# Layer 1's products of the last 64 tokens, in three groups over four PSUM banks

## The chip, the cores and the metric

The kernel runs on one core of a Trainium2 chip. The metric is the device time of one execution in microseconds (us). The engines are TensorE (PE, with its weight loads written PEld), VectorE (DVE), ScalarE (ACT), GpSimd (POOL) and SyncE (SP, which here issues most of the DMAs).

## The reference

Four layers follow each other on an input of 4 x 56 x 56 x 256 numbers in fp32; each adds to its input what it computes from the group-normalised input. Layers 0, 2 and 3 are forms of windowed attention and aren't touched. Layer 1 takes each image's 3136 pixels as tokens:

```python
xn = x / jnp.maximum(jnp.linalg.norm(x, axis=-1, keepdims=True), EPS)
A = jnp.einsum('bnc,cc,bmc->bnm', xn, W_adj, xn)
A = jnp.exp(5.0 * (A - jnp.max(A, axis=-1, keepdims=True)))
A = A * (1.0 - jnp.eye(n, dtype=A.dtype))
A = A / jnp.maximum(jnp.sum(jnp.abs(A), axis=-1, keepdims=True), EPS)
...
AxW = jnp.einsum('bnc,dc->bnd', Ax, W_aff)
diff = rowsum * (xW + b_aff) - AxW
```

A layer norm and a leaky ReLU of `diff` follow. The sum over all pairs of tokens is the bulk of the work: 3136 x 3136 logits, their exponentials, and the product of these with the values, for each of four images.

## The kernel before

**Tiles and symmetry.** The 3136 tokens are 24 tiles of 128 (`NB`) and a rest of 64 (`REST`). The matrix of exponentials is symmetric, so only tiles with j <= i are computed, and each block serves twice: transposed, as a part of row j's sum (the "row product"), and as it stands, as a part of row i's sum (the "column product"). The values `xw` have 257 columns, the last of them -1, so that the same product gives the sum of the weights. Row j's sum stays in a PSUM bank for the whole row; column products go each to a bank of its own and are added at once to `acc` in SBUF by `add_up` (L1562 to L1567): the first one into a tile is copied, by DVE or ACT, and later ones are added by DVE.

**The rest.** The last 64 tokens have their own three units an image, `q` = 0, 1, 2, each against eight tiles. `rest_logits` (L1570) puts the logits of 64 tokens against two groups of four tiles on the two halves of the partitions: `a` = 0 on partitions 0 to 63, `a` = 1 on 64 to 127. `rest_transposed` (L1589) transposes the four 128 x 128 blocks into bank t, from which ACT copies them to `at`. `rest_products` (L1597) then does, for each i of 0 to 3, two column products (one for each half, on 64 rows of the array, written 64*128 in the profile, L1603), their addition, and two row products (on 64 columns of the array, 128*64, L1607), which build up both halves of the bank `po`. For q = 2 a product of the rest with itself follows (`own`, L1611). `po` is added to `racc` (L1613, L1615).

**PSUM.** [...]`psum_tile(tag, bufs)` (L872) gives the next of `bufs` buffers under a tag; a matmul into a buffer waits until the readers of its last use are through. In layer 1 the eight banks are: s (logits, 2), t (transposes, 1), v (column products, 2), o (row products, 2) and m (1, by `ps_m`), which the smaller steps of tokens, statistics and output use.

**What sets the order.** A list of `units` (L1733 and after) holds the blocks of each row, four tiles at a time, with the rest units put in: q = 0 and q = 1 of image 0 at the very start and of the later images between rows 20 and 22 of the image before; q = 2 after row 0 of its own image. The main loop (L1793) does for each unit: a small step (`small_step`, which is one of lengths, values, output transposes, statistics), the transposes, the next unit's logits (`begin`), another small step, then the products. `tick` (L1554), called between products, emits one of the pending steps of normalisation (`normal`, `leaky`, the next image's tokens), mostly on DVE. In layer 1 PE and DVE execute in the order in which the code emits (`manual_schedule`, engines PE and DVE); a scheduler orders ACT's, POOL's and SP's lists.[...]

## Time and profile before

| | |
|---|---|
| median of 3 runs | 3770.52 us (3767.21 to 3772.34) |
| the profiled execution | 3769.93 us, span 3768.0 us |
| layer 1, about | 734 to 2600 us |
| PE busy in it (734 to 2600) | 1852.76 of 1866.00 us |
| DVE, ACT, POOL busy in it | 866.46, 420.53, 538.36 us |
| L1603, column products of the rest | 192 records, 377 to 481 ns, median 429 |
| L1607, row products of the rest | 192 records, 380 to 432 ns, median 406 |
| L1567, first copies out of a bank | DVE 64 at 426 ns, ACT 32 at 374 ns (medians) |
| L1564, additions to `acc` | DVE 1104 at 423 ns (median) |

The span runs from the first to the last instruction. Each fp32 product is two records on PE. [...]records of matmuls that follow each other overlap; the distance from start to start is what a product takes up of PE. In brackets after a row stands how long its engine had nothing to do before it, and whose end ended that.

### The profile page before, as it was taken

The page shows a single profiled execution, that of the slowest core. Times are in us where ns is not written, and L with a number is a line of the kernel's source. Part 1 is how long each engine was busy: PE and PEld are TensorE (multiplying, and loading weights), DVE is VectorE, ACT ScalarE, POOL GpSimd, SP SyncE. Part 2 cuts the span into 40 slices and gives each one's busy share as a digit, 9 for nine tenths or more (in the row PEclk, how much of TensorE's full clock was granted, in tenths as well). Part 3 has the DMA queues.
Part 4 walks back from the last instruction along what each step waited for, and adds up shares of the span by engine and source line. Part 5 has one row for each costly group of instructions (what it writes and reads, how often), then busy time and mean ns, then how long its engine had stood idle before and what let it go on. Part 6 is the DMA issues. An engine that isn't in the chain of part 4 may idle for free. (4 is left out here: it accounts for less than half of the span.)

```text
span 3768.0 us, 112324 instructions
## 1 busy us (share of the span) xinstructions
PE 3665.8 (97%) x48826; PEld 2478.1 (66%) x48826; DVE 2200.9 (58%) x4188; ACT 1472.2 (39%) x3125; POOL 1815.9 (48%) x1966
## 2 busy tenths in 40 slices
PE   8999999999999999999999999999999999999998
PEld 4555556677776777767777667775666666555554
DVE  5777777634445444464344544445676777777676
ACT  5565566422222222222222222222666666444443
POOL 4777777612235222352222421123777777555555
PEclk9999999999999999999999999999999999999999
DMA  6544444300010000011000000002544444534443
GB/s 213 169 153 134 132 123 137 134 7 23 23 27 29 22 19 18 21 32 28 19 16 22 26 20 10 11 20 78 138 133 137 132 128 119 155 126 139 130 134 99
DMA packets 278039, 304.94 MB, mean 81 GB/s; under 512 B 33624, under 2 KB 268764, under 8 KB 277084
## 3 DMA queue, kind: packets, MB, share of 16 engines
q1 hardware_dynamic: 275680, 297.43, 25.7%
q8 instruction: 385, 6.31, 0.7%
q0 software_dynamic: 1568, 0.16, 0.1%
q14 instruction: 118, 0.97, 0.1%
q10 hardware_dynamic: 288, 0.08, 0.0%
HBM read 205.04 MB, written 92.55 MB: 79 GB/s over the span
## 5 line engine op out<-in xcount | busy, mean ns | idle before, releaser
L1564 DVE TENSOR_TENSOR acc<-acc,ps_v 128x257 f32<-128x257 f32 x1104 | 463.8, 422 | 781.8 <-PE ps_v L1642 753.4
L1642 PE MATMUL ps_v<-xw,e 128*128 128x257 f32 x2208 | 611.0, 381 | 3.4 <-DVE xnT L1509 2.2
L1637 PE MATMUL ps_o<-xw,at 128*128 128x257 f32 x2208 | 609.0, 379 | 0.0
L1532 PE MATMUL ps_s<-xnT,xd 128*128 128x512 f32 (+3 forms) x1344 | 571.4, 548 | 3.9 <-DVE xnT L1509 3.9
L1626 ACT COPY at<-ps_t 128x512 f32<-128x512 f32 (+3 forms) x332 | 170.6, 514 | 960.9 <-PE ps_t L1623 960.7
L1642 PEld LDWEIGHTS ps_v<-xw,e 128*128 128x128 f32 x2208 | 413.4, 189 | 144.6 <-issue 83.2
L1087 POOL TENSOR_TENSOR b<-e 126x336 f32<-126x336 f32 (+5 forms) x512 | 499.5, 997 | 7.7
L1637 PEld LDWEIGHTS ps_o<-xw,at 128*128 128x128 f32 x2208 | 419.1, 190 | 60.1
L952 PE MATMUL ps_m<-xn,w_wqkv 128*32 128x392 f32 x4096 | 376.4, 496 | 8.0 <-ACT gst L917 3.4
L1525 POOL TENSOR_SCALAR xd<-xnT,vec 128x128 f32<-128x128 f32 x192 | 116.4, 616 | 478.0 <-PE ps_s L1532 477.8
L1078 POOL TENSOR_TENSOR e<-e,m0t 126x672 f32<-126x672 f32 (+3 forms) x128 | 238.8, 1865 | 182.1 <-ACT e L1077 180.6
L1535 ACT ACTIVATE e<-ps_s 128x512 f32<-128x512 f32 x336 | 185.4, 552 | 355.0 <-PE ps_s L1532 351.8
L1532 PEld LDWEIGHTS ps_s<-xnT,xd 128*128 128x128 f32 x1344 | 225.4, 191 | 141.4 <-issue 126.2
L1078 POOL TENSOR_TENSOR e<-e,bias 119x784 f32<-119x784 f32 (+5 forms) x128 | 239.4, 1870 | 157.3 <-ACT e L1077 156.9
L1096 PEld LDWEIGHTS ps_o<-e,vp 124*32 124x32 f32 (+3 forms) x8192 | 200.3, 110 | 101.9 <-issue 84.1
L998 ACT ACTIVATE no<-rs 128x168 f32<-128x168 f32 (+2 forms) x256 | 94.0, 367 | 426.0 <-DVE rs L1960 190.2
L952 PEld LDWEIGHTS ps_m<-xn,w_wqkv 128*32 128x32 f32 x4096 | 123.8, 110 | 183.1 <-issue 128.6
L1960 DVE RECIPROCAL rs<-ps_o 128x196 f32<-128x196 f32 (+2 forms) x128 | 175.7, 1372 | 109.7 <-PE ps_o L1096 108.0
L1096 PE MATMUL ps_o<-e,vp 124*32 124x112 f32 (+3 forms) x8192 | 232.2, 249 | 3.1 <-POOL e L1078 2.5
L1075 ACT ACTIVATE e<-e 126x672 f32<-126x672 f32 (+5 forms) x256 | 219.7, 858 | 13.3 <-DVE e L1074 1.9
L1077 ACT ACTIVATE e<-ps_s 126x672 f32<-126x672 f32 (+5 forms) x256 | 206.3, 806 | 5.4 <-PE ps_s L1067 3.0
L979 PE MATMUL ps_m<-w_wqkv,xn 128*32 128x256 f32 x3136 | 196.9, 381 | 2.1 <-DVE v L983 1.6
(214 smaller groups left out, 5945.5 us busy)
## 6 DMA issues: line engine op xcount, KB each, us to landing
x<-xr SPq DMA_DIRECT2D x64, 392.0 KB
x<-in_x SPq DMA_DIRECT2D x53, 448.0 KB
x<-x SPq DMA_DIRECT2D x60, 392.0 KB
xr<-x SPq DMA_DIRECT2D x60, 392.0 KB
vd<-v SPq DMA_DIRECT2D x72, 256.0 KB
xr<-in_x SPq DMA_DIRECT2D x32, 392.0 KB
xr<-x SPq DMA_DIRECT2D x28, 448.0 KB
x<-xr SPq DMA_DIRECT2D x28, 448.0 KB
```

The costliest lines, as they stand in the source:

```text
L952: nc.tensor.matmul(pm[j * HD:(j + 1) * HD, :n], lhsT=w[:, h, col + j * HD:col + (j + 1) * HD], rhs=rhs(h), start=(h == 0), stop=(h == CC - 1))
L979: nc.tensor.matmul(pm[i:i + HD, j * C:(j + 1) * C], lhsT=xn[:, h, first + i:first + i + HD], rhs=w[:, h, :], start=(h == 0), stop=(h == CC ...
L1075: nc.scalar.activation(ev, ev, AF.Exp)
L1077: nc.scalar.activation(ev, sv, AF.Exp)
L1078: nc.gpsimd.tensor_tensor(parts(ev), parts(ev), w["emask"], ALU.mult)
L1087: nc.gpsimd.tensor_tensor(w["b"][a][:nk, :, :2 * nq].rearrange("p h (i c) -> p h i c", i=2), ev[:, :, :, 0, :], ev[:, :, :, 1, :], ALU.add)
L1096: nc.tensor.matmul(w["o"](k, i)[j * HD:(j + 1) * HD], lhsT=ones[:nk, :HD] if k else v(j, u), rhs=w["b"][j // 2][:nk, j % 2, i * nq:(i + 1) ...
L1532: nc.tensor.matmul(s[:, :n], lhsT=xd[j][:, h, :], rhs=xnT[:, h, first * P:last * P], start=(h == 0), stop=(h == CC - 1))
L1535: nc.scalar.activation(e[:, :n], s[:, :n], AF.Exp, scale=5.0)
L1564: nc.vector.tensor_tensor(acc[:, i, :], acc[:, i, :], pv[:, :C + 1], ALU.add)
L1637: nc.tensor.matmul(out[j][:, :C + 1], lhsT=e[:, col(i)] if i == j else at[:, col(i)], rhs=xw[:, i, :], start=(i == j), stop=(i == NB - 1))
L1642: nc.tensor.matmul(pv[:, :C + 1], lhsT=e[:, col(i)], rhs=xw[:, j, :], start=True, stop=True)
```

## The change

`rest_products` alone is changed. Before, its order is, four times: two column products into the two v banks, their additions, two row products, a tick. After, it is: the column products of tiles i = 0 (into both v banks) and i = 1 (`a` = 0 into bank t, `a` = 1 into bank m), the four additions; all eight row products, with a tick after the second and the fourth pair; the column products of i = 2 (into t and m) and i = 3 (into v), their four additions; two ticks. The number of products, additions and ticks is the same, and so is every result's place.

```diff
         def rest_products(b, q, e, own, at):
             po = psum_tile("o", 2)
+
+            def by_column(i, banks):
+                for a, bank in enumerate(banks):
+                    pv = psum_tile(*bank)
+                    half = slice(a * REST, (a + 1) * REST)
+                    nc.tensor.matmul(pv[:, :C + 1], lhsT=e[half, i * P:(i + 1) * P], rhs=xw[half, NB, :], start=True, stop=True)
+                    found.append((i, a, pv))
+
+            def add():
+                for i, a, pv in found:
+                    add_up(b, 8 * q + 4 * a + i, pv, (nc.vector.tensor_copy, nc.scalar.copy)[a])
+                found.clear()
+
+            found, pair, others = [], [("v", 2)] * 2, [("t", 1), ("m", 1)]
+            by_column(0, pair)
+            by_column(1, others)
+            add()
             for i in range(4):
-                pv = [psum_tile("v", 2) for a in range(2)]
-                for a in range(2):
-                    half = slice(a * REST, (a + 1) * REST)
-                    nc.tensor.matmul(pv[a][:, :C + 1], lhsT=e[half, i * P:(i + 1) * P], rhs=xw[half, NB, :], start=True, stop=True)
-                for a in range(2):
-                    add_up(b, 8 * q + 4 * a + i, pv[a], (nc.vector.tensor_copy, nc.scalar.copy)[a])
                 for a in range(2):
                     nc.tensor.matmul(po[a * REST:(a + 1) * REST, :C + 1], lhsT=at[:, i * P + a * REST:i * P + (a + 1) * REST],
                                      rhs=xw[:, 8 * q + 4 * a + i, :], start=(i == 0), stop=(i == 3 and (a == 1 or own is None)))
+                if i % 2:
+                    tick()
+            by_column(2, others)
+            by_column(3, pair)
+            add()
+            for _ in range(2):
                 tick()
             if own is not None:
```

## The prediction

> **What bounds the kernel now.** First the page: its parts 1 and 2 say that TensorE (PE) is busy nearly throughout, and part 5 puts the layer in question between the products on L1637 and L1642. The chain of waits on the page reaches back only into layer 3, so it doesn't speak of this stage. I therefore read busy time by stretches: layer 1 runs from about 734 to 2600 us.

> ```profile
> span 3768.0 us, 112324 instructions
> ...
> PE 3665.8 (97%) x48826; PEld 2478.1 (66%) x48826; DVE 2200.9 (58%) x4188; ACT 1472.2 (39%) x3125; POOL 1815.9 (48%) x1966
> ```

> The busy times of two stretches of layer 1 (microseconds, and records in brackets):

> ```profile
> core 0: us, PE busy (x) PEld busy (x) DVE busy (x) ACT busy (x) POOL busy (x), PEclk, DMA share, GB/s
> 734.00:800.00 66.00, 65.08 (x311) 40.35 (x310) 23.88 (x62) 21.16 (x41) 12.59 (x21) 1.00 0.27 106
> 800.00:1190.00 390.00, 389.27 (x1719) 292.95 (x1719) 178.45 (x460) 86.56 (x160) 115.94 (x165) 1.00 0.09 24
> ```

> In 800 to 1190 us PE is busy 389.27 of 390.00 us, and DVE, the next engine, 178.45. So the stage is PE's queue played back to back: a microsecond taken out of it brings the end forward by a microsecond, provided that no other engine comes within reach. The changed code stands twelve times in it (three units for each of four images: 192 records on L1603 at 16 a unit).

> Next I read the timeline of such a unit. This is the first of image 1 (start, length, engine, line, count, and in brackets the idle time before it with its releaser):

> ```profile
> 1189.84 0.70 PE L1603 MATMUL ps_v<-xw,e 64*128 64x257 f32 x4
> 1190.47 0.20 PEld L1607 LDWEIGHTS ps_o<-xw,at 128*64 128x64 f32 x4 [0.33 <-ACT e L1535]
> 1190.48 0.65 PE L1607 MATMUL ps_o<-xw,at 128*64 128x257 f32 x4
> 1190.58 0.43 DVE L1567 COPY acc<-ps_v 128x257 f32<-128x257 f32 x1 [0.23 <-PE ps_v L1603]
> 1190.62 0.38 ACT L1567 COPY acc<-ps_v 128x257 f32<-128x257 f32 x1 [0.18 <-PE ps_v L1603]
> 1191.06 0.30 PEld L1603 LDWEIGHTS ps_v<-xw,e 64*128 64x128 f32 x4 [0.39 <-DVE acc L1567]
> 1191.06 0.70 PE L1603 MATMUL ps_v<-xw,e 64*128 64x257 f32 x4
> ```

> A pair of column products (tiles 64*128) takes from 1189.84 to 1190.48, 0.63 us; the pair of row products (128*64) from 1190.48 to 1191.06, 0.58. Before each the weight load sits idle 0.33 to 0.39 us. Four rounds of 1.22 make the unit 4.88 us. "PE busy" hides this[...].

> How much of it is work? The undivided products give the pace:

> ```profile
> 755.46 0.59 PE L1642 MATMUL ps_v<-xw,e 128*128 128x257 f32 x2
> ...
> 755.89 1.03 PE L1637 MATMUL ps_o<-xw,at 128*128 128x257 f32 x4
> ```

> Two more records cost 1.03 - 0.59 = 0.44, so one of 257 columns costs about 0.215. A product is two records, and two half-array tiles run side by side: a pair needs 2 x 0.215 = 0.43. What remains, 0.20 for a column pair and 0.15 for a row pair, is paid at each alternation. That pairs of one kind do follow each other without it is seen where the last tokens' logits run:

> ```profile
> 735.55 1.94 PE L1574 MATMUL ps_s<-xnT,xdr 128*64 128x512 f32 x8
> ```

> Eight records of 512 columns at 0.43 each would take 3.44 in a row; they take 1.94, that is four slots of 0.43 and one 0.22.

> [...]

> **The change part by part.** Durations are from the one profiled execution: span 3768.0 us, its own time 3769.93, which is 0.6 under the median of 3770.52; I take savings off the median.

> 1. Alternations. Before: eight groups a unit, 4 x 0.63 + 4 x 0.58 = 4.84 (seen: 4.88). After: columns, rows, columns: 16 slots x 0.215 = 3.44, and three starts, 0.20 + 0.15 + 0.20: 3.99. Saved 0.89 a unit, twelve times: 10.7 us. Nothing is recomputed; the number of matmuls is the same. Unknown: whether column pairs on 64 rows follow each other at 0.215, since before never has two in a row. Their weight loads take 0.18 each, but both tiles' run together (four in 0.30 in the row above), so a slot of 0.215 covers them. Bounds: nothing lost, or 0.1 for each of five joints, 6.0 us in all.[...] I take zero.

> 2. Waits inside a unit that the change removes. From first column to the next other instruction, the twelve units take 67.1 us by the timeline, of which 12 x 4.88 is the rhythm above and 4 x 0.58 the product with `own` (L1611). The other 6.2 are waits:
>    - The third unit of each image (6.09 us instead of 5.46) adds all columns on DVE. The second and fourth columns wait for it twice, 0.31 each: "DVE acc L1564: 4.6, 12" among the releasers of L1603. With four banks, two pairs are emptied under the four row pairs (1.87 us): at 0.38 each the four adds, begun at 0.73, end at 2.3, and y's step on L1696 (0.41) at 2.7, while the banks are wanted at 2.93. Saved 4 x 0.63 = 2.5.
>    - The second unit of image 0 (6.21 us) waits 1.33 for ACT, which is filled from 744.28 to 751.56 with exponentials of layer 2's bias (L1849, 1.0 each). In the new order on ACT, m's first copy has one of these before it and should end near 748.2; its bank is wanted at 745.41 + 2.93 = 748.34. But m's and v's last copies come behind three more, near 751.9, and the next unit's second column wants v about then. I take 1.0 back of 1.33 (bounds 0 and 1.33).
>    - The second units of images 1 to 3 wait 0.74 at their second product for ACT's copy of `xw` (L961) out of v. That stays: 0.

> 3. Waits that the change adds. Bank t has one buffer, and so has m.
>    - At the end: the second group begins with t and m, and the next instruction on PE writes t (the transposes on L1623) or m. Column start to DVE's copy is 0.73, the copy 0.43, and 0.06 to PE: free at 1.22, wanted at 2 x 0.43 + 0.20 = 1.06. That is 0.16 behind which all PE waits, in eight units (the four with `own` have 0.58 more in between): 1.3 us. DVE is free in time: the steps moved between the copies (L945 0.60, L1701 0.55) end before 2.9 and t's copy comes at 3.66.
>    - At the beginning: t was emptied long before (L1594 ends some 0.5 us ahead of the unit, with another 0.53 before t's second use). m is late in the first unit, where ACT reads the statistics (L916, L917) until 738.5, wanted at 737.74 + 0.53: 0.3. In the first units of images 1 to 3 DVE's L1716 frees m at 1190.34, wanted at 1190.37: 0.
>    Together 1.6. Bounds: 0, where PE would not have been ready, and 1.1 per unit, 13, if each ACT copy of m stood behind an instruction of 1.06 us as in the second unit.

> 4. The rest. The tick steps move from after each tile to two in the middle and two at the end; PE and DVE keep the order in which the code emits. By the instruction lists of both kernels, SP and POOL, and so all DMA issues, keep their order; ACT's list differs by a copy to `at` that moves ahead of a square of 1.06 us (L1470). I cost this at nothing: ACT is idle 0.84 before most of its copies, and that cover gone would cost 0.4 a unit, already within the bound of 3.

> Sum: 10.7 + 2.5 + 1.0 - 1.6 = 12.6 us. 3770.5 - 12.6 = 3757.9; the profiled execution would be 3757.3. Layers 2 and 3 only begin earlier.

> **The rivals.**
> - *All of it comes*: no end waits (+1.3), the second unit's rest, and room downstream. 67.1 less 12 x 3.99 and 4 x 0.58 is 16.9: 3753.6. For it: PE bound. Against: the 0.74 on `xw` and the copy's 1.22 are in the trace.
> - *The joints don't close, or banks give part back*: 6.0 lost at the joints leaves 6.6, 3763.9; with as much again lost on t and m, 3770. For it: no row shows two row-tiled pairs in a row. Against: L1574 and the loads that run together.
> - *Slower: bank m behind ACT.* The second group's m product waits for ACT's copy of the first[...]. It decides from 1.05 us a unit on (12.6 / 12) and gives 0.2% slower from 1.7. At two bias exponentials a unit (2.0): 3757.9 + 24 = 3782. For it: the second unit has such a queue. Against: in the others ACT waits for the columns, not they for it.

> **How the numbers follow.** About 0.2%, 7.5 us, is what a measurement of this kernel can tell from no change. The forecast (3755 to 3761) 0.66; all of it 0.10; part given back (3761 to 3770) 0.20, of which 0.08 still faster by over 7.5; slower 0.04. Hence faster 0.84, same 0.12, slower 0.04. The range 3753.6 to 3764 takes in the first rival's end and the joints' bound.

> **What would show it.** Units near 4.15 us (4.6 with `own`), t's wait for DVE of about 0.16 ahead of the transposes, the weight load's idle time before row products once a unit instead of four times, layer 1 shorter by 12 to 13 us and layers 2 and 3 of the same length. I am wrong if column pairs in a group stand 0.5 or more apart, if releasers of the columns name ACT in most units, or if units shrink and PE idles by as much elsewhere.

## The result and the profile after

The changed kernel takes 3757.49 us (median of 7 runs, 3754.05 to 3760.45) against 3770.9 (7 runs) on the same chip: a ratio of 0.9965, 95% interval 0.9955 to 0.9974. That is 13 us, with an interval of 10 to 17. The forecast was 3757.9.

The page of the changed kernel, and then the busy times of stretches of layer 1:

```profile
span 3752.2 us, 112327 instructions
...
PE 3649.2 (97%) x48826; PEld 2480.3 (66%) x48826; DVE 2195.6 (59%) x4188; ACT 1471.4 (39%) x3125; POOL 1813.6 (48%) x1966
```

```profile
734.00:800.00 66.00, 65.86 (x327) 44.93 (x324) 25.75 (x69) 21.52 (x42) 12.30 (x20) 1.00 0.20 82
800.00:1180.00 380.00, 379.27 (x1678) 286.03 (x1677) 174.16 (x448) 83.64 (x154) 114.19 (x163) 1.00 0.09 24
```

The share of PE's busy time is what it was, 97%, and in the middle of layer 1 it idles 0.73 us as before. The number of PE records is the same. So the share tells nothing of the change; 16 us of "busy" have gone with the span.

Not all of these 16 us are the change's. I measure layer 1 in both traces from the first transposes of the rest (L1593) to the last logits (L1532): 1862.8 us before and 1850.8 after, 12.0 less. Layer 0, whose code is the same, took 735.0 and 730.9, and what follows layer 1 took 1170.3 and 1170.6. The traces' record of the granted clock has PE at half speed for 20.5 us of layer 0 before and 13.7 after; half of the difference, 3.4, is most of those 4.1 us. The traces of the experiments below bear this out: over all ten, this time runs from 10.2 to 23.9 us and the length of layer 0 with it, from 730.7 to 736.5. In layer 1 neither trace has such a stretch. Hence the length of layer 1 is a far sharper measure than the whole time, and I use both below.

The same unit as was shown of before, the first of image 1, PE's rows of the timeline:

```profile
1181.88 0.70 PE L1604 MATMUL ps_v<-xw,e 64*128 64x257 f32 x4
1182.41 0.38 PE L1604 MATMUL ps_t<-xw,e 64*128 64x257 f32 x1
1182.44 0.48 PE L1604 MATMUL ps_m<-xw,e 64*128 64x257 f32 x1
1182.63 0.38 PE L1604 MATMUL ps_t<-xw,e 64*128 64x257 f32 x1
1182.76 0.38 PE L1604 MATMUL ps_m<-xw,e 64*128 64x257 f32 x1
1183.06 1.96 PE L1618 MATMUL ps_o<-xw,at 128*64 128x257 f32 x16
1184.95 0.48 PE L1604 MATMUL ps_t<-xw,e 64*128 64x257 f32 x1
...
1185.28 0.38 PE L1604 MATMUL ps_t<-xw,e 64*128 64x257 f32 x1
...
1185.49 0.60 PE L1604 MATMUL ps_v<-xw,e 64*128 64x257 f32 x4
1186.17 0.44 PE L1640 MATMUL ps_t<-ident,e 128*128 128x128 f32 x2
```

The second column pair begins 0.53 after the first, the row products are one block of 1.89 us, start to start, and the unit ends after 4.29 instead of 4.88. Two small waits are to be seen, and the weight loads of this unit show both:

```profile
1182.20 0.40 PEld L1604 LDWEIGHTS ps_t<-xw,e 64*128 64x128 f32 x2
1182.43 0.29 PEld L1604 LDWEIGHTS ps_m<-xw,e 64*128 64x128 f32 x2
...
1184.95 0.18 PEld L1604 LDWEIGHTS ps_t<-xw,e 64*128 64x128 f32 x1 [0.39 <-issue]
...
1185.28 0.41 PEld L1604 LDWEIGHTS ps_v<-xw,e 64*128 64x128 f32 x4
1186.17 0.20 PEld L1640 LDWEIGHTS ps_t<-ident,e 128*128 128x128 f32 x2 [0.48 <-DVE acc L1567]
```

In the first group the weights for t are loaded from 1182.20, 0.2 ahead of t's first product; those for m only from 1182.43, together with m's first product, since DVE's L1733 reads m until 1182.38. That product's record takes 0.48 where t's takes 0.38, the two tiles run askew, and the group is 0.12 longer. And the transposes begin 1.22 after the start of the last column group, about 0.15 later than that group needs (1.06, in a run below). The releaser of their weight load is DVE's copy out of t. Over all units, the idle time before the column products no longer names the additions. Of the releasers of L1603 in the kernel before, "DVE acc L1567: 7.9, 20", "DVE acc L1564: 4.6, 12" and "ACT acc L1567: 0.8, 2" are gone, and what is left is (line L1604, source view):

```profile
its engine sat idle before it (us, times) until:
  issue: 6.4, 16
  DVE mv L1707: 2.4, 4
  DVE mv L1708: 2.3, 3
  ACT xw L961: 1.4, 3
```

This is weaker evidence than it looks. 7.9 / 20 and 4.6 / 12 are 0.38 to 0.40, the time that the weight load idles before every lone column pair; "issue" has 0.40 a time as well, with no copy named. So these lines counted alternations, and named the copy that happened to end last.

From first column to the next other instruction, the twelve units now take 54.7 us, against 67.1: 12.4 less, where layer 1 is 12.0 shorter.

### The profile page after: what moved, and what is told of

The parts are those of the page before. It is cut to its first block, busy times and chain, and to the rows that moved or that the text cites. A ratio compares the mean times of both kernels' runs of the same rounds, so it can differ in the third digit from the quotient of the medians.

```text
span 3752.2 us, 112327 instructions
## 1 busy us (share of the span) xinstructions
PE 3649.2 (97%) x48826; PEld 2480.3 (66%) x48826; DVE 2195.6 (59%) x4188; ACT 1471.4 (39%) x3125; POOL 1813.6 (48%) x1966
## 5 line engine op out<-in xcount | busy, mean ns | idle before, releaser
L1564 DVE TENSOR_TENSOR acc<-acc,ps_v 128x257 f32<-128x257 f32 x1088 | 457.4, 422 | 774.9 <-PE ps_v L1659 752.0
L1532 PE MATMUL ps_s<-xnT,xd 128*128 128x512 f32 (+3 forms) x1344 | 571.4, 548 | 3.9 <-DVE xnT L1509 3.9
L1535 ACT ACTIVATE e<-ps_s 128x512 f32<-128x512 f32 x336 | 185.3, 552 | 354.1 <-PE ps_s L1532 350.8
L1532 PEld LDWEIGHTS ps_s<-xnT,xd 128*128 128x128 f32 x1344 | 225.3, 191 | 141.4 <-issue 126.2
```

What stands on the lines that cost most here:

```text
L1532: nc.tensor.matmul(s[:, :n], lhsT=xd[j][:, h, :], rhs=xnT[:, h, first * P:last * P], start=(h == 0), stop=(h == CC - 1))
L1535: nc.scalar.activation(e[:, :n], s[:, :n], AF.Exp, scale=5.0)
L1564: nc.vector.tensor_tensor(acc[:, i, :], acc[:, i, :], pv[:, :C + 1], ALU.add)
```

## Experiments

Two readings of the result were open. The theory is that each change between row tiles (64*128) and column tiles (128*64) costs PE 0.15 to 0.20 us, and the grouping removes five of eight per unit. The rival is that in the kernel before a round of 1.22 us is just as long as v's emptying takes (0.73 to DVE's copy, 0.43 for it, 0.06 back to PE), so that the four banks, and not the grouping, could be what helped. The table has the outcome of all runs; "units" is the sum of the twelve, and ratios are to the kernel before as measured together with each: its median was 3770.9 us beside the changed kernel, 3768.1 beside the next four rows, 3769.4 beside "m held, 12 copies" and "ACT empties t", and 3770.1 beside the last two. Units and layer 1 are from one trace of each kernel. Wherever two column pairs follow each other here, they have four banks; that they need four wasn't shown.

| kernel | units, us | layer 1, us | median, us | ratio, 95% interval |
|---|---|---|---|---|
| before | 67.1 | 1862.8 | | |
| changed | 54.7 | 1850.8 | 3757.5 | 0.9965 (0.9955 to 0.9974) |
| alternating, four banks | 63.0 | 1858.7 | 3763.4 | 0.9992 (0.9983 to 1.0) |
| four groups | 55.7 | 1851.4 | 3757.2 | 0.9968 (0.9957 to 0.9979) |
| three groups, spare banks | 51.5 | 1847.6 | 3756.1 | 0.997 (0.9957 to 0.9982) |
| two groups | 49.5 | 1845.2 | 3750.1 | 0.9952 (0.9939 to 0.9966) |
| m held, 12 copies | | 1902.2 | 3803.3 | 1.0083 (1.0066 to 1.01) |
| ACT empties t | 55.6 | 1851.3 | 3757.9 | 0.9972 (0.9963 to 0.9982) |
| m held, 7 copies | | 1867.9 | 3774.5 | 1.0009 (1.0003 to 1.0016) |
| two groups, t by DVE | 49.1 | 1844.8 | 3754.1 | 0.9954 (0.994 to 0.9967) |

Where no bank is held on purpose, layer 1's length follows the sum of the units to within 0.5 us.

**The old order with four banks.**

```diff
-            by_column(0, pair)
-            by_column(1, others)
-            add()
             for i in range(4):
+                by_column(i, (pair, others)[i % 2])
+                add()
...
-                if i % 2:
-                    tick()
-            by_column(2, others)
-            by_column(3, pair)
-            add()
-            for _ in range(2):
                 tick()
```

> The order of before (a column pair, a row pair, four times), but with the columns of tiles 1 and 3 in banks t and m, so that no pair waits for v's emptying. Theory (the alternation of half-array modes costs 0.15 to 0.20 us each, and is 10.7 of the 12.6 us): a unit stays near 4.88 us, the units with DVE additions fall from 6.09 to about 5.45; the twelve sum to about 63 us, against 67.1 before and 54.7 after; time about 3767. Rival (it was the wait for v: 0.73 to DVE's copy, 0.43 copy, 0.06 back is 1.22, just the old round): a unit falls to 4.0 to 4.2, sum near 55, time about 3758.

Measured: units 63.0 us, layer 1 4.1 us shorter than before, ratio 0.9992. The plain units keep 4.87 or 4.88 us; those whose columns are all added by DVE fall from 6.09 to 5.45. The third unit of image 0:

```profile
785.48 0.70 PE L1604 MATMUL ps_v<-xw,e 64*128 64x257 f32 x4
786.11 0.65 PE L1617 MATMUL ps_o<-xw,at 128*64 128x257 f32 x4
786.69 0.48 PE L1604 MATMUL ps_t<-xw,e 64*128 64x257 f32 x1
...
787.01 0.38 PE L1604 MATMUL ps_t<-xw,e 64*128 64x257 f32 x1
...
787.33 0.65 PE L1617 MATMUL ps_o<-xw,at 128*64 128x257 f32 x4
787.91 0.70 PE L1604 MATMUL ps_v<-xw,e 64*128 64x257 f32 x4
788.55 0.65 PE L1617 MATMUL ps_o<-xw,at 128*64 128x257 f32 x4
```

With no bank to wait for, the pairs still stand 0.63 and 0.58 apart. The rival falls as the cause of the round's length: the two limits happened to coincide at 1.22, and with the wait gone the alternation alone upholds it. The banks by themselves are worth 4.1 of the 12.0 us, by the removed waits; the rest needs the grouping.

**Four groups: columns of two tiles, rows of two, twice.**

```diff
             for i in range(4):
+                if i % 2 == 0:
+                    by_column(i, pair)
+                    by_column(i + 1, others)
+                    add()
```

> Columns of two tiles, rows of two, columns of two, rows of two. Theory: 16 slots of 0.215 and four starts (0.20, 0.15, 0.20, 0.15) make 4.14 us a unit, with no wait for t or m at the end since rows come last; sum 12 x 4.14 + 4 x 0.58 + 3 x 0.74 (copy of xw) + 0.3 = 54.5 us, the same as the changed kernel within 1 us, time 3757. Rival (an alternation costs far more when banks are full, or the first additions come too late for the second columns at 2.07 us): sum of 58 or more, time 3761 or more.

Measured: units 55.7, 1.2 more than expected; layer 1 0.6 longer than after. The units with DVE additions take 4.75, or 4.17 without `own`, where 4.14 was expected. The surplus is mostly m's lateness at the beginning (0.12 to 0.38, as in the changed kernel) and 0.34 in the second unit of image 0, whose second columns wait for bank m: ACT's copy out of it stands behind a bias exponential and ends at 747.88, and m's products start at 747.94 instead of beside t's at 747.71. One more alternation a unit and no wait at the end come out even, as the theory said; the rival's 58 is excluded.

**Three groups over banks that nobody else wants.**

```diff
-            found, pair, others = [], [("v", 2)] * 2, [("t", 1), ("m", 1)]
-            by_column(0, pair)
-            by_column(1, others)
+            found, pair, others = [], [("v", 2)] * 2, [("t", 1), ("s", 2)]
+            by_column(0, others)
+            by_column(1, pair)
...
-            by_column(2, others)
+            by_column(2, [("s", 2)] * 2)
```

> Three groups as in the change, but the first begins with banks t and s and then v, and the second uses both s banks and then v; m is not used, and neither t nor m is wanted at the end. Theory: the waits that the change added (0.16 at the end, m at the beginning) and 0.44 of the 0.74 for the copy of xw go: 12 x 3.99 + 4 x 0.58 + 3 x 0.3 = 51.1 us against 54.7, time about 3754. Rival (PE would have waited there for something else, the exponentials or the copy to at): the units shrink but the next instructions stand later by as much, layer 1 as long as after, time 3757.

Measured: units 51.5, layer 1 3.2 us shorter than after. The first unit of image 1 again:

```profile
1182.65 0.48 PE L1604 MATMUL ps_t<-xw,e 64*128 64x257 f32 x1
...
1183.72 1.96 PE L1618 MATMUL ps_o<-xw,at 128*64 128x257 f32 x16
1185.61 0.70 PE L1604 MATMUL ps_s<-xw,e 64*128 64x257 f32 x4
1186.14 0.60 PE L1604 MATMUL ps_v<-xw,e 64*128 64x257 f32 x4
1186.67 0.44 PE L1640 MATMUL ps_t<-ident,e 128*128 128x128 f32 x2
```

It takes 4.02 us by these rows, and the transposes start 1.06 after the last group. Of the 3.2 us, about 1.2 are the wait for t or m at the end of eight units, 0.7 m at the beginning, and 1.2 a part of the wait for the copy of `xw` in the second units of images 1 to 3 (4.33 instead of 4.90). So these waits of the changed kernel were real and PE had nothing else to wait for. In the time the 3 us don't show: the ratio, 0.997, can't be told from the change's.

**Two groups: all columns, then all rows.**

```diff
-            found, pair, others = [], [("v", 2)] * 2, [("t", 1), ("m", 1)]
-            by_column(0, pair)
-            by_column(1, others)
-            add()
+            found, banks = [], [[("t", 1), ("s", 2)], [("m", 1), ("o", 2)], [("v", 2)] * 2, [("s", 2), ("t", 1)]]
+            for i in range(4):
+                by_column(i, banks[i])
+                if i % 2:
+                    add()
             for i in range(4):
...
-                if i % 2:
-                    tick()
-            by_column(2, others)
-            by_column(3, pair)
-            add()
-            for _ in range(2):
                 tick()
```

> All eight column products first, over t and s, m and o, v and v, s and t again, then all eight row products. Theory: two starts only, 16 x 0.215 + 0.20 + 0.15 = 3.79 us a unit; sum 12 x 3.79 + 4 x 0.58 + 0.5 = 48.3 us, time about 3751. Rival (the banks reused within the group, or by the next unit, are emptied too slowly: DVE and ACT have four copies each, DVE eight in the last unit of an image): the gain over the change goes into waits, sum near 54, time 3757.

Measured: 3750.1 us, ratio 0.9952, units 49.5, layer 1 5.6 us shorter than after. Units without a wait take 3.82. PE's first and last rows of the first unit of image 1:

```profile
1181.29 0.48 PE L1604 MATMUL ps_t<-xw,e 64*128 64x257 f32 x1
...
1182.38 0.60 PE L1604 MATMUL ps_v<-xw,e 64*128 64x257 f32 x4
...
1183.34 1.96 PE L1619 MATMUL ps_o<-xw,at 128*64 128x257 f32 x16
1185.23 0.44 PE L1635 MATMUL ps_t<-ident,e 128*128 128x128 f32 x2
```

The series of units without waits is 4.88 for eight groups, 4.17 for four, 4.03 for three, 3.82 for two: from eight to two 1.06 us, 0.18 for each alternation. The step from four to three leaves out the start of a row group (0.14), that from three to two the start of a column group (0.21), near the forecast's 0.15 and 0.20. Not all of this kernel's gain over the changed one is of this kind: 2.2 of the 5.2 us that the units lose is the wait for the copy of `xw` in the second units of images 1 to 3, where v isn't wanted until the third pair. This kernel has the lowest median, and its layer 1 is shorter than the changed kernel's; the intervals of the two ratios still overlap.

Where the 0.14 to 0.21 lie can be read from the rows. A column pair by itself takes two slots of 0.32 (786.69, 787.01 and 787.33 in the old order with four banks) instead of 0.215. The first slot of a group is long: its weight load begins with it (1184.95 in the changed kernel, for both), while inside a group the weights are loaded a slot ahead (1185.28 for the products from 1185.49 on). The last is long too: the first load of the other shape begins only together with its product (both at 1183.06 in the changed kernel, after 0.33 us without a load, 0.30 after the start of m's last column product at 1182.76). Why it begins no earlier wasn't shown; what was measured is the 0.14 to 0.21 us.

**The two groups with t emptied by DVE.**

```diff
-            found, banks = [], [[("t", 1), ("s", 2)], [("m", 1), ("o", 2)], [("v", 2)] * 2, [("s", 2), ("t", 1)]]
+            found, banks = [], [[("t", 1), ("s", 2)], [("m", 1), ("o", 2)], [("v", 2)] * 2, [("t", 1), ("s", 2)]]
```

> The two groups again, with t as the bank of half 0 in the last column pair, so that DVE and not ACT empties it both times. Theory: only the second unit of image 0 changes, where ACT's copy of t stood behind the exponentials: its 4.34 us fall to about 3.9 and layer 1 by some 0.4 us, which the time cannot show: 3750. Rival (t is then free too late inside the group, since its first copy by DVE ends at 1.22 and it is wanted at 1.28): the column group of every unit grows by 0.1 or more, layer 1 by over 1 us.

Measured: that unit falls from 4.34 to 3.98, the others keep theirs, layer 1 is 0.4 shorter, and the time (0.9954 against 0.9952) shows no difference. The rival, a longer column group in every unit, falls.

**Who empties t.** The engines of the first copies are exchanged in the changed kernel.

```diff
-                    add_up(b, 8 * q + 4 * a + i, pv, (nc.vector.tensor_copy, nc.scalar.copy)[a])
+                    add_up(b, 8 * q + 4 * a + i, pv, (nc.scalar.copy, nc.vector.tensor_copy)[a])
```

> The changed kernel with the first copies exchanged: ACT empties the banks of half 0 (t among them), DVE those of half 1 (m among them). Theory: where ACT has nothing else, its copy starts 0.04 later and is 0.05 shorter than DVE's, so the end wait of 0.16 stays; in the second unit of image 0, t's last copy stands behind three exponentials of layer 2's bias, and the next transposes wait some 2 us for it; layer 1 is 1 to 2.5 us longer than after, all of it at that unit; time about 3759. Rival (which engine empties t doesn't matter because ACT's queue is short everywhere): layer 1 as after within 0.3 us.

Measured: layer 1 0.5 us longer than after, less than expected. The second unit of image 0 is where it happens, but it grows by 0.82 and not by 2:

```profile
748.34 0.55 PE L1640 MATMUL ps_t<-ident,e 128*128 128x128 f32 x3 [0.90 <-ACT acc L1567]
```

The three exponentials on ACT run from 745.09 to 748.03. They begin 1.2 us before the second column group (746.30), so that most of their length passes while PE is still at that unit's products; t's copy, behind them, begins at 747.90. The mechanism is right, its size was not; the rival's 0.3 us is passed as well.

**m held, to find where the slower rival decides.** The same numbers are copied to the same place twelve times more, and nothing else is changed:

```diff
                 for i, a, pv in found:
+                    for _ in range(12 if (i, a) == (1, 1) and q < 2 else 0):
+                        nc.scalar.copy(acc[:, 8 * q + 4 * a + i, :], pv[:, :C + 1])
                     add_up(
```

> The changed kernel with twelve more copies of m's first product by ACT, in the eight units of q = 0 and q = 1: the same numbers are copied to the same place again, so that m stays taken. It asks from where on the rival of bank m behind ACT decides. Theory: m's copies begin at 1.2 us of a unit, and thirteen of them at 0.24 to 0.38 us apart end at 4.5 to 6.1, where the second group wants m at 2.96: PE stands still for 1.5 to 3.1 us in each of eight units, layer 1 is 12 to 25 us longer than after, time 3769 to 3782, and the first 1.3 us of delay cost nothing. Rival (PE isn't bound there, or other matmuls pass the waiting one): layer 1 grows by less than half of what m is held, time below 3765.

Measured: ratio 1.0083, layer 1 51.4 us longer than after, twice the upper end. Only a part of it is m's lateness: m's second products begin 3.52 us later after the first column than in the changed kernel in seven units and 5.86 in the second of image 0, 30.5 in all. (The copies came 0.40 us apart, and the forecast's longest distance was 0.38.) In these 30.5 PE is idle for 24.2, for t's two products still run before m's (waits of PE, in us, times and longest):

```profile
PE ps_m L1604 <- ACT acc L1567: 24.2, 8, 4.5
```

The other 20.9 come with a slower clock. The stretches around one such wait, the granted clock in the third column from the end:

```profile
1197.00:1201.00 4.00, 4.00 (x28) 2.15 (x26) 2.36 (x8) 3.12 (x8) 2.75 (x5) 1.00 0.00 0
1201.00:1204.00 3.00, 0.17 (x3) 0.12 (x2) 0.43 (x1) 2.62 (x7) 0.00 (x0) 0.84 0.00 0
1204.00:1206.00 2.00, 2.00 (x7) 1.16 (x8) 0.81 (x3) 0.38 (x2) 0.00 (x0) 0.50 0.00 0
```

In each of the eight waits (2.82 or 2.83 us, one of 4.47), or up to 1.1 us after it, the clock falls to half and stays there for 6.83 us, 54.6 in all. PE has work in 50.8 of them; half of that, 25.4, is an estimate of the loss if PE never waited for anything else, and 20.9 are found. The trace of the changed kernel has no such stretch in layer 1.

The same with seven copies:

> As the run with m held by twelve more copies, with seven of them (the same numbers to the same place). There the copies came 0.40 us apart, and PE's granted clock fell to half for 6.8 us after each idle stretch of about 3 us. Theory: eight copies of 0.40 from 1.2 on free m at 4.4, so PE idles about 1.4 us in each of six units and about 2.5 in the two of image 0[...]; with 0.2 more a unit for the m and t products that no longer run side by side, layer 1 is 13 to 17 us longer than after, and no half-speed stretch stands in it: time 3770 to 3774, the gain used up. Rival (the clock falls after any wait of over 1 us): half-speed stretches in layer 1 again, and 20 us or more.

Measured: ratio 1.0009 (1.0003 to 1.0016), layer 1 17.2 us longer than after, at the upper end. In seven units m comes 1.5 us later than in the changed kernel, and they grow by 1.3 to 1.5, nearly one for one, as the theory had it; PE is idle for 0.79 of that, while t's products fill the rest. Their clock stays full. In one, the second of image 0, the theory fails: with ACT's exponentials added PE idles 4.1 and not 2.5, and the clock falls to half for 6.8 us. The rival, a fall of the clock after any wait of over 1 us, isn't reached by the seven waits of 0.79, but other waits of layer 1 settle it. Three idle stretches of 1.31 us stand in it before and after the change and with m held by twelve or seven copies, in the changed kernel these (waits of PE as above; the first ends at 1239.60):

```profile
PE ps_s L1532 <- DVE xnT L1509: 3.9, 3, 1.3
```

In the kernels before and after the granted clock is 1.00 from 734 to 2560 us, and so around these. So the rival falls, and between 1.31 and 2.82 us of waiting these runs show nothing in layer 1.

## Why the prediction was right

**Step 1, alternations: right, a little too large.** The unit without waits is 4.03 (three groups over spare banks), not 3.99, so 0.85 are saved a unit and 10.2 us instead of 10.7. The unknown was settled at the value taken: column pairs inside a group follow at 0.21 to 0.22 where their banks are free (in the two groups v's pair follows at 1182.38 on m's second slot at 1182.16).

**Step 2, waits removed: right for the DVE units, too small in image 0.** The old order with four banks shows 0.64 a unit for the four (6.09 to 5.45), as reckoned from 0.31 twice. But the line that it took for these waits, "DVE acc L1564: 4.6, 12", is not them: it counts the 0.39 before the weight loads of three column pairs a unit. The waits themselves stand inside the second and fourth pair, one of which takes 1.02 where one without a wait takes 0.70:

```profile
787.71 0.70 PE L1603 MATMUL ps_v<-xw,e 64*128 64x257 f32 x4
...
788.93 1.02 PE L1603 MATMUL ps_v<-xw,e 64*128 64x257 f32 x4
```

In the second unit of image 0 all of the 1.33 came back instead of 1.0: from its first column to that of the third unit it is 42.30 us before and 40.97 with the old order over four banks. ACT's late copies of m and v begin at 746.45 and 746.71 in the changed kernel, and the next column products into v at 747.68: they were not late enough to be waited for. The 0.74 on `xw` stayed in all three units, as was said.

**Step 3, waits added: right mechanism, one place missed.** At the end 0.15 for t instead of 0.16. At the beginning 0.38 in the first unit instead of 0.3, and 0.12 in the first units of images 1 to 3, costed at 0. The prediction compared the time at which m comes free with the start of m's product; but m's weight load would have run 0.2 earlier, beside t's, and it waits too. In all about 1.9 us for 1.6.

**Step 4, nothing for the rest: right.** The units lose 12.4 us and layer 1 12.0, so that 0.4 come back elsewhere in it, and the layers behind it kept their length.

The sum, 10.2 + 2.5 + 1.3 - 1.9 = 12.1, is near layer 1's 12.0; the forecast's 12.6 had errors of both signs, and that it came so close is in part luck. The signs that it named came: units of 4.17 (4.60 with `own`), t's wait for DVE, and the shorter layer 1. The rival of the lost joints fell with the trace. The slower rival was real in kind: with m held by seven copies the gain is more than used up, at a mean of 17.2 / 12 = 1.4 us a unit; one for one it is used up at 12.0 / 12 = 1.0, and the rival had put this point at 1.05. But its price, one for one, was seen only for the short delay of 1.5 us; one of 3.5 cost 6.0 to 6.3. In the changed kernel nothing stands before ACT's copies of m that would bring it there.

## What to carry to other kernels

Where small products of two tile shapes alternate on PE, put all of one shape together: each alternation cost about 0.18 us here, and busy time doesn't show it (97% before and after); compare the distances from start to start with the pace of an undivided product. Before crediting a gain to grouping or to added banks, run the old order with the new banks, since a wait for a bank and an alternation can have the same length. Choose the banks of a group by who wants them next: with all columns first, over banks that are free at that moment, the wait at the end goes, v is wanted later, and two alternations suffice. What stays is m, where it comes free late at the beginning. To learn when a bank is wanted, look at the weight load and not at the product: the changed kernel's load for m, in the unit shown, began at 1182.43, 0.05 after DVE had read m, where t's began at 1182.20, 0.2 ahead of its product.

## What the runs showed of the hardware that was not expected

ACT's repeated copies of 128x257 numbers from one bank to one and the same place came 0.40 us apart (twelve in 4.85), while its copies out of m and v to different places in the changed kernel begin 0.26 apart (746.45 and 746.71), though each is 0.37 to 0.41 long.
